# Batch 1's largest logits: VectorE 32x32 squares and five small transfers in place of TensorE transposes and a product with ones

## The chip, the core and the metric

The kernel runs on one core of a Trainium2 chip, with all arithmetic in float32. The metric is the device time in microseconds (us) of one execution, as the median of several runs. Profiles are of one execution; their times start at the beginning of its span.

## What is computed

The reference is four layers on two batches of 1024 tokens of 256 numbers: a cross-attention, a grouped feed-forward layer, a second cross-attention with sigmoids, and a "soft mixture" layer. The change lies in the last one, which in short is:

```
logits   = einsum("bsd,etd->bset", xn, se)        # 1024 tokens x 1024 slots for each batch
dispatch = softmax(logits, axis=1)                # over the tokens
slots    = einsum("bsd,bset->betd", xn, dispatch)
h        = gelu(slots @ w1);  processed = h @ w2
combine  = softmax(logits over all slots, axis=-1)
out      = processed weighted with combine;  x = x + out
```

The softmax over the tokens needs, for every slot, the largest logit of all 1024 tokens of its batch. The logits lie with tokens in partitions, so this is a maximum across partitions, and the result has to be in every partition, since each token's row is reduced by it.

## The kernel before, in words

A batch's 1024 tokens are 8 tiles of 128 tokens. For each tile `logits(b, s)` (line 211) makes 128 x 1024 logits in two PSUM banks on TensorE (L223). VectorE writes their negatives to SBUF (`lg`, L231) and keeps a running elementwise maximum over the tiles (`rmax`, 128 x 1024, L238 and L242). ScalarE makes the exponentials `ec` for the combine step (L246).

After the last tile of a batch `rmax` still holds 128 rows. `largest(b)` (line 289) turns it on TensorE, 8 transposes of 128 x 128 into two banks (`pm`, L295), takes the maximum of each row of the turned squares on VectorE (L296), and writes `dg` on VectorE: eight diagonal 128 x 128 matrices, side by side, with the maxima on the diagonals (L300). `spread(b)` (line 308) multiplies `dg` by a matrix of ones on TensorE (`pb`, L314), which puts the maxima into all partitions, and copies the two banks to `mb`, one half by ScalarE (L170) and one by VectorE (L172).

Then for each tile `less(b, s)` (line 318) adds `mb` to the negative logits on GpSimd (POOL), and `dispatch(b, s)` (line 321) takes the exponential on ScalarE. `gather(b, c)` (line 326) multiplies the exponentials of 128 slots (column `c`) by the tokens: 8 tiles in two passes each, 16 TensorE passes to a column (`psl`, L330). VectorE divides by the sum (`rz`, L338, and `sl`, L340). `turn_slots` (line 343) transposes these slots on TensorE (`pst`, L349), and `slots_out` writes pairs of columns to `slT` (L357). `hidden(b)` runs the first weights and the gelu with seven products in place of eight (L405; its first copy on ScalarE is L438, its first sum on VectorE L445), `processed(b)` the second weights (`pp`, L475), `combined(b)` the combine step (`pc`, L475).

The order of the work: batch 0's `largest`, `spread`, `less` and `dispatch` lie among batch 1's logits. Batch 1's lie after the last logits, where `less(1, c)` and `dispatch(1, c - 1)` are traced with column `c` of batch 0's gather. Batch 1's exponentials are first read by batch 1's gather. `sum_weights` (line 367, four sums on POOL, L373 to L376) prepares the first weights. `turn(q, h)` (line 257) turns halves of `ec` for the combine step: four VectorE transposes in 32 x 32 squares (L275) and 16 transfers on SP's queue (L284). The weights `ms` (2 MB) are loaded on SP's queue (L1270) into memory that becomes free when the logits are done.

A scheduler puts each engine's instructions in order before the run, by readiness in its own model and by order of tracing. The order is then fixed, and an instruction whose input isn't there holds up all behind it on its engine. ScalarE's order is that of the program (L1237). `tc.keep_in_program_order(ins)` pins one instruction behind the instruction of the same engine that was traced before it.

Pools have named memory: tiles of one pool with the same `tag` share it. `slp` has one buffer of the tag `slT`.

Of the kernel before, what the change touches and what calls it, by code (L numbers as in the profile page):

```python
# [9 lines left out]
FP = mybir.dt.float32  # L10
AF = mybir.ActivationFunctionType
ALU = mybir.AluOpType
AX = mybir.AxisListType
PSUM = bass.MemoryType.PSUM

P = 128
# [3 lines left out]
DC = D // P  # L20
# [21 lines left out]
NSLOT = 1024  # L42
# [3 lines left out]
SQ = 32  # L46
R4 = P // SQ
# [3 lines left out]
def tile_kernel(  # L51
# [19 lines left out]
    nc = tc.nc  # L71

    const = ctx.enter_context(tc.tile_pool(name="const", bufs=1))
    stat = ctx.enter_context(tc.tile_pool(name="stat", bufs=4))

    ps = [
        ctx.enter_context(tc.tile_pool(name=f"ps_{i}", bufs=4, space=PSUM)) for i in range(2)
# [2 lines left out]
    def bank(name, side=0):  # L80
        return ps[side].tile([P, 512], FP, tag="bank", name=name)
# [69 lines left out]
    keep, pools = {}, {}  # L151
# [12 lines left out]
    lgs = [[None] * ST for _ in range(B)]  # L164
    ecs = {}
    rmaxs, zcs, mTs, mbs = {}, {}, {}, {}

    def copy(engine, dst, src):
        if engine == 0:
            nc.scalar.copy(dst, src)  # L170
        else:
            nc.vector.tensor_copy(dst, src)  # L172
# [84 lines left out]
    def turn(q, h, late=False):  # L257

        if q < QB:
            tr = pools["m12"].tile(
                [P, R4, EC // 2, QT, SQ], FP, tag="tr", name=f"tr_{q}_{h}", bufs=2
            )
        else:

            if h == 0:
                trs[q] = keep[0].tile(
                    [P, 2, R4, EC // 2, QT, SQ], FP, tag=f"ec_{q % QB}", name=f"tr_{q}"  # L270
                )
            tr = trs[q][:, h]
        half = ecs[q][:, h]
        for t in range(QT):
            ins = nc.vector.transpose(  # L275
                tr[:, :, :, t, :].rearrange("p r c n -> p c r n"),
                half[:, t, :].rearrange("p (c r n) -> p c r n", c=EC // 2, r=R4),
            )
            if late:
                tc.keep_in_program_order(ins)  # L280
        to = half.rearrange("p a b -> p (a b)").rearrange("p (k i n) -> p k i n", i=R4, n=SQ)
        for i in range(R4):
            for r in range(R4):
                nc.sync.dma_start(  # L284
                    out=to[ts(r, SQ), :, i, :],
                    in_=tr[ts(i, SQ), r].rearrange("p c t n -> p (c t) n"),
                )

    def largest(b):

        mT = stat.tile([P, EC], FP, tag="mT", name=f"mT_{b}")
        for h in range(EC // 4):
            pm = bank(f"pm_{b}_{h}", 1)
            for c in range(4):
                nc.tensor.transpose(pm[:, ts(c, P)], rmaxs[b][:, ts(4 * h + c, P)], ident)  # L295
            nc.vector.tensor_reduce(  # L296
                mT[:, ts(h, 4)], pm.rearrange("p (c n) -> p c n", c=4), AX.X, ALU.max
            )
        dg = pools["mw"].tile([P, EC, P], FP, tag="dg", name=f"dg_{b}")
        nc.vector.tensor_tensor(  # L300
            dg,
            ident.unsqueeze(1).to_broadcast([P, EC, P]),
            mT.unsqueeze(2).to_broadcast([P, EC, P]),
            ALU.mult,
        )
        mTs[b] = dg

    def spread(b):

        dgf = mTs[b].rearrange("p c n -> p (c n)")  # L310
        mb = pools["md"].tile([P, NSLOT], FP, tag="mb", name=f"mb_{b}")
        for n in range(NSLOT // 512):
            pb = bank(f"pb_{b}_{n}", 1)
            nc.tensor.matmul(pb, lhsT=ones, rhs=dgf[:, ts(n, 512)], start=True, stop=True)  # L314
            copy(n, mb[:, ts(n, 512)], pb)
        mbs[b] = mb

    def less(b, s):
        nc.gpsimd.tensor_tensor(lgs[b][s], lgs[b][s], mbs[b], ALU.add)  # L319

    def dispatch(b, s):
        nc.scalar.activation(lgs[b][s], lgs[b][s], AF.Exp, scale=-1.0)  # L322
# [3 lines left out]
    def gather(b, c):  # L326

        pz = bank(f"psl_{b}_{c}", 0)
        for s in range(ST):
            nc.tensor.matmul(  # L330
                pz[:, 0:XW],
                lhsT=lgs[b][s][:, ts(c, P)],
                rhs=xhs[b * QB + s // QT][:, s % QT, :],
                start=(s == 0),
                stop=(s == ST - 1),
            )
        rz = stat.tile([P, 1], FP, tag="rz", name=f"rz_{b}_{c}")
        nc.vector.reciprocal(rz, pz[:, D : D + 1])  # L338
        sl = pools["m12"].tile([P, D], FP, tag="sl", name=f"sl_{b}_{c}", bufs=2)
        nc.vector.tensor_scalar(sl, pz[:, 0:D], rz, None, ALU.mult)  # L340
        sls[c] = sl

    def turn_slots(b, c):

        if c % 2 == 0:
            pts[c // 2] = bank(f"pst_{b}_{c // 2}", 1)
        pt = pts[c // 2]
        for dc in range(DC):
            nc.tensor.transpose(  # L349
                pt[:, ds(dc * 2 * P + (c % 2) * P, P)], sls[c][:, ts(dc, P)], ident  # L350
            )
        if c % 2 and c < EC - 1:
            for dc in range(DC):
                slots_out(b, c // 2, dc)
# [12 lines left out]
    def sum_weights():  # L367
        m1s = m12s[0]
        a11, a12 = m1s[:, 0, 0:512], m1s[:, 1, 0:512]
        a21, a22 = m1s[:, 0, 512:], m1s[:, 1, 512:]  # L370
        st = const.tile([P, DC, NSLOT], FP, tag="seT", name="m1_sums")
        s1, s2, s4 = st[:, 0, 0:512], st[:, 0, 512:], st[:, 1, 0:512]
        nc.gpsimd.tensor_tensor(s1, a21, a22, ALU.add)  # L373
        nc.gpsimd.tensor_tensor(a21, a11, a21, ALU.subtract)
        nc.gpsimd.tensor_tensor(s2, s1, a11, ALU.subtract)
        nc.gpsimd.tensor_tensor(s4, a12, s2, ALU.subtract)  # L376
        lefts.extend([a11, a12, s4, a22, s1, s2, a21])
# [310 lines left out]
    with (  # L688
# [349 lines left out]
        with (  # L1038
# [136 lines left out]
            for q in range(NQ):  # L1175
                b = q * QN // S
# [63 lines left out]
    for u in range(1, B * ST + 2):  # L1240
        b, s = divmod(u, ST)
        if b < B:
            if u in (1, 3):
                norm_tokens(QB + u // 2)
                turn_tokens(QB + u // 2)
            logits(b, s)
        v = u - ST
        if v == 1:
            nc.vector.reciprocal(zcs[0], zcs[0])
            largest(0)  # L1250
        if v == 2:
            spread(0)
        if 2 <= v < 2 + ST:
            less(0, v - 2)
        if 3 <= v < 3 + ST:
            dispatch(0, v - 3)
# [1 line left out]
    nc.vector.reciprocal(zcs[1], zcs[1])  # L1258


    largest(1)
    spread(1)
    work.close()
    m12 = open_pool("m12")
    ms = m12.tile([P, DC * FF + OC * D], FP, name="ms")
# [5 lines left out]
    for b in range(B):  # L1271
        slTs[b] = pools["slp"].tile([P, DC, NSLOT], FP, tag="slT", name=f"slT_{b}")
        for c in range(EC):
            gather(b, c)
            if c > 0:
                turn_slots(b, c - 1)
            if b == 0 and c in (1, 3, 5):
                turn(c // 4, c // 2 % 2, c == 5)
            if b == 1 and c % 2 == 0:
                turn(QB + c // 4, c // 2 % 2, True)  # L1280
            if b == 0:
                less(1, c)
                if c > 0:
                    dispatch(1, c - 1)
        if b == 0:
            dispatch(1, ST - 1)
            sum_weights()
        hidden(b)
        with tc.manual_schedule(engines={mybir.EngineType.DVE, mybir.EngineType.PE}):
            processed(b)  # L1290
            combined(b)
# [70 lines left out]
```

## Time and profile before

| | |
|---|---|
| Median of three runs | 444.54 us (443.05 to 444.97) |
| Time of the profiled execution | 443.19 us |
| Its span | 441.4 us |
| TensorE busy (PE) | 430.4 us, 97% |
| VectorE busy (DVE) | 328.4 us, 74% |
| ScalarE busy (ACT) | 114.7 us, 26% |
| GpSimd busy (POOL) | 84.7 us, 19% |
| TensorE's granted clock | 0.999 |
| Logits of both batches, TensorE (L223) | 128 passes, 593 ns each |
| `psl` (L330) | 256 passes, 381 ns each, overlapping |
| `less` on POOL (L319) | 16, 2361 ns each |
| `dispatch` on ScalarE (L322) | 16, 1049 ns each |
| Batch 1's `less` | first one starts at 234.06, last one ends at 252.67 |
| First hidden copy on ScalarE (L438) | 259.98 |

PE is TensorE's products, PEld its weight loads, DVE VectorE, ACT ScalarE, SP the engine that issues the transfers. A line of a timeline gives start, length, engine, line of the kernel, operation, output and inputs, shapes and the number of instructions merged; in brackets stands the idle time before it and what ended it. The chain of waits starts at the last instruction and goes back, at each step, to what released it; a line is start, length and work. A row of a transfer ends in the median time from issue to landing.

### The profile page before, as it was taken

To read this page: it belongs to the slowest core of one execution; us is meant where nothing else is said; L and a number is where in the kernel's file an instruction comes from. 1 tells how busy PE (TensorE), PEld (TensorE's weight loads), DVE (VectorE), ACT (ScalarE), POOL (GpSimd) and SP (SyncE) were. 2 spreads that over 40 slices of the span, in tenths; PEclk is the share of its full clock that TensorE was granted. 3 is DMA by queue.
4 is the path that set the end of the run, shared out by engine and by line. 5 is a ranking of instruction groups with operands and counts; after the bars stand their busy time and mean duration, and the time that the engine had idled before them with its cause. 6 is when DMAs were issued, how large, how long until landed. Compare 5 with 4: busy or idle time off the path is not lost.

```text
span 441.4 us, 6412 instructions
## 1 busy us (share of the span) xinstructions
PE 430.4 (97%) x2368; PEld 319.1 (72%) x2368; DVE 328.4 (74%) x735; ACT 114.7 (26%) x213; POOL 84.7 (19%) x84
## 2 busy tenths in 40 slices
PE   6999999999999999999999999999999999999996
PEld 5788898888645545444458864699998884499996
DVE  0587989899284787998787259995995568796956
ACT  1212334112345441343573405510000002530000
POOL 3012232234212111200887930000000000000000
PEclk9999999999999999999999999999999999999999
DMA  8996595400202132321043633332003666600002
GB/s 269 415 422 274 224 379 206 170 0 7 42 10 39 21 47 30 48 32 18 0 162 72 98 52 50 45 56 43 1 0 103 97 90 99 90 1 1 1 1 97
DMA packets 100641, 42.08 MB, mean 95 GB/s; under 512 B 94593, under 2 KB 96769, under 8 KB 99201
## 3 DMA queue, kind: packets, MB, share of 16 engines
q1 hardware_dynamic: 100610, 41.67, 35.4%
q8 instruction: 19, 0.31, 0.3%
q14 instruction: 12, 0.10, 0.1%
HBM read 28.03 MB, written 2.10 MB: 68 GB/s over the span
## 4 chain that ended last, share of the span: by engine, by line
PE 81%; DVE 15%; POOL 1%; ACT 1%; issue 1%; DMA 1%; ACTq 0%; POOLq 0%
PE psl L330 12%; PE pl L223 12%; PE pp L475 11%; PE pc L475 11%; PE pmh L405 11%; PE pmt L744 5%; DVE b2z L775 5%; PE pq L1120 3%; PE pf L1134 3%; PE psg L1187 2%; PE poT L1221 2%; PE po L802 2%; DVE hn_f L708 1%; DVE bn_f L113 1%; DVE bn_a L113 1%; PE pt_a L125 1%
## 5 line engine op out<-in xcount | busy, mean ns | idle before, releaser
L744 PE MATMUL pmt<-wg 128*128 128x256 f32 x256 | 58.9, 388 | 3.8 <-DMA wg<-in_wff_dram 3.8
L330 PE MATMUL psl<-xh,lg 128*128 128x258 f32 x256 | 58.7, 381 | 0.0
L744 PEld LDWEIGHTS pmt<-wg 128*128 128x128 f32 x256 | 49.2, 195 | 10.7 <-DMA wg<-in_wff_dram 4.1
L223 PE MATMUL pl<-seT,xhT 128*128 128x512 f32 x128 | 55.9, 593 | 0.0
L330 PEld LDWEIGHTS psl<-xh,lg 128*128 128x128 f32 x256 | 47.3, 190 | 7.1 <-issue 0.5
L223 PEld LDWEIGHTS pl<-seT,xhT 128*128 128x128 f32 x128 | 24.2, 190 | 29.1 <-issue 24.9
L319 POOL TENSOR_TENSOR lg<-lg,mb 128x1024 f32<-128x1024 f32 x16 | 37.2, 2361 | 30.8 <-DVE mb L172 30.8
L475 PEld LDWEIGHTS pp<-ms,mh 128*128 128x128 f32 x256 | 29.4, 192 | 1.0 <-issue 1.0
L475 PE MATMUL pp<-ms,mh 128*128 128x128 f32 x256 | 29.7, 276 | 0.0
L246 ACT ACTIVATE ec<-lg,nm 128x1024 f32<-128x1024 f32 x16 | 18.4, 1148 | 40.4 <-DVE nm L231 40.4
L775 DVE SCALAR_TENSOR_TENSOR b2z<-wg,fr,b2z 128x256 f32<-128x256 f32 x48 | 24.6, 516 | 0.5
L415 ACT ACTIVATE mh<-mh 128x512 f32<-128x512 f32 x32 | 19.2, 627 | 20.3 <-DVE mh L448 17.7
L405 PE MATMUL pmh<-slT,ms 128*128 128x512 f32 x48 | 24.0, 592 | 0.0
L475 PE MATMUL pc<-pr,ec 128*128 128x128 f32 x192 | 22.1, 275 | 0.0
L475 PE MATMUL pp<-m_sums,mh 128*128 128x128 f32 x192 | 22.1, 275 | 0.0
L338 DVE RECIPROCAL rz<-psl 128x1 f32<-128x1 f32 x16 | 2.5, 156 | 26.0 <-PE psl L330 26.0
L475 PEld LDWEIGHTS pc<-pr,ec 128*128 128x128 f32 x192 | 21.8, 192 | 0.0
L475 PEld LDWEIGHTS pp<-m_sums,mh 128*128 128x128 f32 x192 | 21.8, 192 | 0.0
L1196 ACT ACTIVATE sg<-psg 128x512 f32<-128x512 f32 x32 | 16.5, 603 | 17.0 <-PE psg L1187 17.0
L275 DVE STREAM_TRANSPOSE tr<-ec 128x512 f32<-128x512 f32 x32 | 20.1, 679 | 0.0
L322 ACT ACTIVATE lg<-lg 128x1024 f32<-128x1024 f32 x16 | 16.5, 1049 | 12.4 <-POOL lg L319 12.4
L486 DVE TENSOR_TENSOR mh<-mh,mh 128x1024 f32<-128x1024 f32 x16 | 18.5, 1219 | 1.5 <-PE pp L475 1.5
(187 smaller groups left out, 703.9 us busy)
## 6 DMA issues: line engine op xcount, KB each, us to landing
wg<-in_wff_dram SPq DMA_DIRECT2D x6, 2048.0 KB, 14.3
ec<-tr SPq DMA_DIRECT2D x128, 64.0 KB, 2.3
xT<-in_xT_dram SPq DMA_DIRECT2D x4, 512.0 KB, 12.8
x<-in_x_dram SPq DMA_DIRECT2D x4, 512.0 KB, 15.0
wg<-in_wff_dram SPq DMA_DIRECT2D x2, 1024.0 KB, 10.6
xhT<-tr_m SPq DMA_DIRECT2D x64, 32.0 KB, 2.0
ms<-in_m_dram SPq DMA_DIRECT2D x1, 2048.0 KB, 7.9
out_dram<-x SPq DMA_DIRECT2D x16, 128.0 KB, 1.8
```

The costliest lines, as they stand in the source:

```text
L223: nc.tensor.matmul(pl, lhsT=xhTs[q][:, dc, ts(t, P)], rhs=seT[:, n, dc, :], start=(dc == 0), stop=(dc == DC - 1),)
L246: nc.scalar.activation(ecs[q][:, :, t, :], lg.rearrange("p (h n) -> p h n", h=2), AF.Exp, bias=nm[:, 1:2], scale=-1.0, accum_out=zcs[b][:, ...
L275: ins = nc.vector.transpose(tr[:, :, :, t, :].rearrange("p r c n -> p c r n"), half[:, t, :].rearrange("p (c r n) -> p c r n", c=EC // 2, ...
L319: nc.gpsimd.tensor_tensor(lgs[b][s], lgs[b][s], mbs[b], ALU.add)
L322: nc.scalar.activation(lgs[b][s], lgs[b][s], AF.Exp, scale=-1.0)
L330: nc.tensor.matmul(pz[:, 0:XW], lhsT=lgs[b][s][:, ts(c, P)], rhs=xhs[b * QB + s // QT][:, s % QT, :], start=(s == 0), stop=(s == ST - 1),)
L405: nc.tensor.matmul(to, lhsT=lefts[i][:, ts(j, P)], rhs=slTs[b][:, i, 0:512] if i < 2 else rights[b][i], start=True, stop=True,)
L415: nc.scalar.activation(h, h, AF.Gelu)
L475: nc.tensor.matmul(to, lhsT=left(k, m), rhs=right[:, k, :], start=(k == 0), stop=(k == QT - 1),)
L486: nc.vector.tensor_tensor(dst, x, y, op)
L744: nc.tensor.matmul(pm[:, ts(hc, D)], lhsT=w1g[:, oc, ts(hc, P)], rhs=w2g[:, oc, :], start=(oc == 0 and hc == 0), stop=(oc == OC - 1 and hc ...
L775: nc.vector.scalar_tensor_tensor(acc, weights[g][1][:, oc, :], b1s[:, g, oc : oc + 1], acc, ALU.mult, ALU.add)
```

## The change

For batch 1 alone `largest` and `spread` are replaced. `largest_by_moves` transposes `rmax` on VectorE in 32 x 32 squares, so that in each block of 32 partitions the partition number stands for the slot within a square; the maximum over the 32 numbers of each square leaves `m1`, 128 x 32. Four transfers bring the four blocks of 32 partitions side by side into 32 partitions (`m4`). `spread_by_moves` takes the maximum over the four (`m2`), turns that 32 x 32 square (`m3`), writes it to DRAM as one row of 1024 numbers, and reads that row into all 128 partitions (`mb`).

The working memory `w` is a tile of the tag `slT`, the one that `slT_0` uses afterwards. `spread_by_moves(1)` is traced in the loop over batch 0's columns behind `gather(0, 0)`; its first reduce is pinned behind the VectorE instruction traced before it. `sum_weights` moves from behind that loop to the same place, ahead of `less(1, 0)`. Of batch 1's `less`, tiles 3 and 6 go to VectorE.

```diff
+    dram = ctx.enter_context(tc.tile_pool(name="dram", bufs=1, space=bass.MemoryType.DRAM))
...
+    moved = {}
+
+    def largest_by_moves(b):
+
+        w = pools["slp"].tile([P, DC, NSLOT], FP, tag="slT", name=f"max_{b}")
+        sq = w[:, 0, :]
+        nc.vector.transpose(sq, rmaxs[b])
+        m1 = w[:, 1, 0:SQ]
+        nc.vector.tensor_reduce(m1, sq.rearrange("p (c k) -> p c k", k=SQ), AX.X, ALU.max)
+        m4 = w[0:SQ, 1, SQ : 5 * SQ].rearrange("n (i c) -> n i c", i=R4)
+        for i in range(R4):
+            nc.sync.dma_start(out=m4[:, i, :], in_=m1[ts(i, SQ), :])
+        moved[b] = w, m4
+
+    def spread_by_moves(b):
+
+        w, m4 = moved[b]
+        m2, m3 = w[0:SQ, 1, 5 * SQ : 6 * SQ], w[0:SQ, 1, 6 * SQ : 7 * SQ]
+        tc.keep_in_program_order(
+            nc.vector.tensor_reduce(m2, m4.rearrange("n i c -> n c i"), AX.X, ALU.max)
+        )
+        nc.vector.transpose(m3, m2)
+        row = dram.tile([SQ, SQ], FP, name=f"mrow_{b}")
+        nc.sync.dma_start(out=row, in_=m3)
+        mb = pools["md"].tile([P, NSLOT], FP, tag="mb", name=f"mb_{b}")
+        nc.sync.dma_start(out=mb, in_=row.rearrange("c n -> (c n)").partition_broadcast(P))
+        mbs[b] = mb
+
     def less(b, s):
-        nc.gpsimd.tensor_tensor(lgs[b][s], lgs[b][s], mbs[b], ALU.add)
+        engine = nc.vector if b == 1 and s in (3, 6) else nc.gpsimd
+        engine.tensor_tensor(lgs[b][s], lgs[b][s], mbs[b], ALU.add)
...
-    largest(1)
-    spread(1)
+    largest_by_moves(1)
     work.close()
...
+            if b == 0 and c == 0:
+                spread_by_moves(1)
+                sum_weights()
             if b == 0:
                 less(1, c)
                 if c > 0:
                     dispatch(1, c - 1)
         if b == 0:
             dispatch(1, ST - 1)
-            sum_weights()
```

## The prediction

> **What bounds the kernel now.** I read the page first, then the chain of waits around the change and behind it, then the timeline of the stretch by engine, and last the rows that carry the costs. The chain says that from the change to the end nothing but TensorE counts:
>
> ```profile
> 225.83 0.02 issue
> 225.86 0.75 DVE lg L231
> ...
> 228.13 0.68 DVE mT L296
> 228.81 0.02 issue
> 228.83 2.26 DVE dg L300
> 231.09 0.04 issue
> 231.14 1.98 PE pb L314 x4
> 233.12 3.49 PE psl L330 x16
> 236.61 0.22 PE pst L349 x2
> ```
>
> ```profile
> 333.62 6.98 PE psl L330 x32
> 340.60 0.22 PE pst L349 x2
> ```
>
> The first fence (start, length, what) is where the chain leaves TensorE: batch 0's gather has begun, but batch 1's maxima go VectorE, `dg`, then TensorE's product with ones. From the last logits' end (225.83) to the first slot transpose (236.61) batch 0 needs 10.78 us; batch 1, with the same 32 passes of `psl` and nothing between, needs 6.98 us. All after 236.61 is TensorE work end to end, so each microsecond saved here moves the end, if nothing new stops TensorE. The timeline of the engines in that stretch:
>
> ```profile
> 225.69 0.63 PE L295 MATMUL pm<-ident,rmax 128*128 128x128 f32 x4
> 226.16 1.47 PE L330 MATMUL psl<-xh,lg 128*128 128x258 f32 x6
> 227.47 0.60 PE L295 MATMUL pm<-ident,rmax 128*128 128x128 f32 x4
> 227.90 2.56 PE L330 MATMUL psl<-xh,lg 128*128 128x258 f32 x10
> 231.14 1.98 PE L314 MATMUL pb<-dg,ones 128*128 128x512 f32 x4 [0.67 <-DVE dg L300]
> 232.96 3.65 PE L330 MATMUL psl<-xh,lg 128*128 128x258 f32 x16
> ```
>
> **What is removed.** On TensorE 8 transposes and 4 passes of `pb` with the idle time before them: at most 10.78 - 6.98 = 3.80 us. On VectorE two reduces, `dg` and half of `mb` (0.68 + 0.69 + 2.25 + 0.69 = 4.3 us), on ScalarE a copy of 0.59. How much of the 3.80 comes out depends on the gather's other input, the exponentials of batch 0:
>
> ```profile
> 227.80 3.88 ACT L322 ACTIVATE lg<-lg 128x1024 f32<-128x1024 f32 x4
> ```
>
> They end at 231.68, the last four 0.97 apart, and are not touched by the change. If TensorE went through column 0 to its end before column 1, it would finish column 0 at 231.68 + 2 x 0.22 = 232.1 and column 1 at 235.6, for a gain of only 1.0. But 16 passes were done by 230.46, before that last exponential, so they can't be all of column 0: the order already mixes columns. Mixed, four passes of tile 7 are left at 231.68, which ends at 232.55, before the 232.81 (225.83 + 6.98) that TensorE needs anyway. I take 0.3 off for imperfect mixing.
>
> **What is added, and when the maxima arrive (T).** VectorE ends its last maximum at 226.53 + 0.68 = 227.2; the reciprocal of `zc` takes 0.2. The 128x1024 square transpose is two rows of L275 (128x512, 0.679) or less, 1.25; the reduce is the row of L861 (128x4 from 128x1024, 1.22). So `m1` is there at 229.9. Four transfers follow on SP's queue. Their issue costs 0.34 each (the row of `ms`) to 0.63 (L284), their landing 2.0 to 2.3:
>
> ```profile
> ec<-tr SPq DMA_DIRECT2D x128, 64.0 KB, 2.3
> xhT<-tr_m SPq DMA_DIRECT2D x64, 32.0 KB, 2.0
> ms<-in_m_dram SPq DMA_DIRECT2D x1, 2048.0 KB, 7.9
> out_dram<-x SPq DMA_DIRECT2D x16, 128.0 KB, 1.8
> ```
>
> `ms` was issued at 225.85, when its memory came free, before `m1` exists, and lands at 233.75; the moves stand behind its bytes: 233.3 at best, 234.6 at worst, I take 234.4. The small reduce and transpose are between 0.16 each (VectorE's 128x4 rows) and 0.68 (a 512-element row); I take 0.5 together, 234.9. The row goes to DRAM in 1.8 to 2.3: 236.9. Reading it back as 128 x 4 KB has no row near: 2.0, and 0.5 MB at (7.9 - 2.0)/2 MB gives 3.5; `bo_bc`, the only like read, took 8.2 in the crowded start. The Trainium skill, "DMA: Bandwidth & Descriptors", section "Anatomy of one DMA", has 2.0 us and bytes over 436 GB/s, which would be 3.2; by the same rule `ms` would take 6.8, the trace shows 7.9, so I stay with the trace. With 0.5 for transfers of `turn` in between, T = 240.9, between 239.5 and 245. The old maxima were there at 233.9. That is 7 us later, and what hides it is that batch 1's exponentials are used first in batch 1's gather at 333.
>
> Three covers have to hold (TensorE's work taken 3.0 earlier than now):
> - The small reduce is pinned behind column 0's slots and waits for the moves until 234.4. Queued behind it are column 1's `rz` and `sl` (0.7), so done by 235.6; TensorE wants them at 239.94 - 3.0 = 236.9. Free; each us after 235.7 costs one. Slots 0 are written into the memory that holds the squares, so they wait for the row's transfer: at 237.9 against 236.9, free as well.
> - POOL now does the weight sums first (252.64 to 257.85, 5.2 us): from 233.75 to 239.0, before T, so free. Then six `less` of 2.33 while VectorE takes two. The last exponential ends at T + 6 x 2.33 + 2 x 1.22 + 1.06 = T + 17.5 = 258.4. ScalarE keeps program order, so the first copy of the hidden layer stands behind it. VectorE needs that copy at 263.88, so it may start as late as 263.25 - 3.0 = 260.2: 1.8 of slack, good up to T = 242.7.
> - Two `less` on VectorE, tiles 3 and 6. Undisturbed 128x1024 sums take 1.22 (L486). But:
>
> ```profile
> L300 DVE TENSOR_TENSOR dg<-ident,mT x2: 1221/1736/2252, 206.3 to 228.8; 128x1024 f32<-128x1024 f32 x2
> ```
>
> The second `dg` took 2.25 because POOL's last `less` ran until 230.0: 1.17 of waiting and 1.22 of work. At 99.80 two POOL sums in a row let one VectorE instruction through between them. The Trainium skill, "SBUF — State Buffer", section "Who interferes with whom", says why: a VectorE instruction with two SBUF inputs and a GpSimd one that reads SBUF share a port, one holding it for its whole instruction. By L486's row a `less` costs VectorE 1.22; by the rule up to 2.33 + 1.22 = 3.55, and the waiting falls on the `rz` and `sl` queued behind. A column's `rz` (244.06 for column 3, its slots wanted at 247.36, 0.7 of work) can slip 2.6 us for nothing. One `less` ahead of column 3 (rz due 241.0, at the latest 243.7) frees VectorE at T + 1.22 or T + 3.55, 242.1 or 244.5: a stall of 0 or 0.8. I take 0.4, and 0.3 for slips of columns 0 to 2.
>
> **Sum.** 3.80 - 0.3 - 0.4 - 0.3 = 2.8 us gained. The profiled execution took 443.19 (span 441.4 and 1.8 around it), which gives 440.4; the median of the three runs is 444.54, so 441.7.
>
> **Rivals.**
> - *Both `less` stand together on VectorE ahead of one column's `rz`* (the slower side). They become ready at the same moment, which speaks for it; against it, columns' `rz` come every 3.7 us and were traced earlier. VectorE is then free at T + 4.8 (it gets the port first) or T + 7.1 (POOL first), 245.7 or 248.0 against the 243.7 that column 3 allows: 2.0 to 4.3 of stall. With 3.5 left of the gain before it, that is -1.5 to +0.8 at my T, and each us of T adds one: with POOL first it is slower than before from T = 240.1 and by 2.2 (0.5%) from T = 242.3, inside the bounds of T; with VectorE first only from 242.4. I price it at POOL first and 242.3: 446.7.
> - *The row or the broadcast is queued behind `turn`'s transfers.* VectorE is idle while it waits, so the 16 transfers of a `turn` may be ready before the row. SP issues one per 0.66 (32 in 21.4 us from 236.85), 16 are 10.6. T would be 251, column 3 stalls 251 + 1.2 + 0.7 - 244.4 = 8.5 or more: 444.5 - 3.5 + 8.5, about 449.5. Against it: the row needs SP before most of them do.
> - *Little comes out*: columns in order (gain 1.0), or the stall of a `less` eats most: 443.5.
>
> **Chances.** Forecast 0.54, 441.7 (its own range 440.5 to 442.8); little 0.22, 443.5; both together 0.15, 446.7; queued behind 0.09, 449.5. The range 440.4 to 446.7 leaves out the last case, half of the third and a little below. A measurement of this kernel tells 0.5% (2.2 us) from no change. Of the forecast 0.45 is under 442.3, with 0.05 of "little" 0.5 faster; the third case splits at its T, so same 0.3, slower 0.2.
>
> **What would show it.** Right: the chain runs from logits to `psl` without `pm` and `pb`; the first 32 `psl` passes end near 233; POOL's first `less` starts near 241; the last exponential ends before 260; `pst` never waits for `sl`. Wrong: idle time of TensorE before `pst` released by VectorE's `sl`, with a `less` of over 2 us on VectorE before it; the broadcast issued after 238; a wait of TensorE or VectorE for the first `mh` copy.

## The result and the profile after

The changed kernel takes 440.76 us (median of six runs, 439.91 to 441.36), the kernel before 444.36 (six runs, 443.05 to 444.97). The ratio is 0.9922 with a 95% interval of 0.9905 to 0.9940, a gain of 2.7 to 4.2 us. The forecast was 441.7. (The title counts five transfers. There are six: four moves, the row to DRAM and its broadcast back.)

Lines below the new functions have moved: `psl` is now L360, `pst` L379, `pmh` L435, `less` L349 on both engines, `slT` L387, and the four sums of slots that the hidden layer's products need L422 to L426. The profiled execution took 441.36, with a span of 439.6; before it was 443.19 and 441.4. In this execution the last logits end at 227.06, 1.23 later than before. That lies at the kernel's start: its first 32 products (`pmt`) took 10.26 us in the place of 8.93. In two later profiles with the change the logits end at 225.93 and 226.07. So times of the two kernels are compared from the end of the logits.

First the chain of waits around the change (start, length, what):

```profile
227.06 8.36 PE psl L360 x38
235.42 0.22 PE pst L379 x2
235.64 2.18 PE psl L360 x10
237.82 0.22 PE pst L379 x2
...
257.44 0.23 PE pst L379 x2
257.68 0.02 issue
257.70 0.88 DVE slT L387 x2
258.57 2.04 DVE sl_sums L422
260.61 0.14 issue
260.75 4.53 PE pmh L435 x10
```

The detour over VectorE, `pm` and `pb` is gone, and TensorE goes from logits to `psl` without a stop. The second `pst` comes 10.76 after the logits (237.82 - 227.06); before it came 14.49 after them. That is 3.73 gained, of at most 3.80. Then, at 257.68, the chain leaves TensorE in a place where it did not before: a sum of slots on VectorE takes 2.04 where such a sum takes 0.68. From the end of the logits to the first product of batch 0's combine step (`pc`) it is 80.49 us, before 82.78: of the 3.73 gained only 2.29 are left. Behind that point nothing differs: from there to the start of VectorE's last instruction it is 129.04 or 129.05 in the profile of before and in each one below.

The points in the kernel before (the second `pst` and the first `pc` of its chain, then the same sum of slots on VectorE's timeline), and the first `pc` of the changed kernel:

```profile
240.32 0.22 PE pst L349 x2
...
308.61 25.01 PE pc L475 x224
```

```profile
260.99 0.68 DVE L392 TENSOR_TENSOR sl_sums<-slT 128x512 f32<-128x512 f32 x1
```

```profile
307.55 25.01 PE pc L505 x224
```

VectorE and POOL in the same stretch (start, length, engine, line, work; in brackets the idle time before and what ended it):

```profile
231.38 2.48 DVE L276 STREAM_TRANSPOSE tr<-ec 128x512 f32<-128x512 f32 x4
...
236.48 0.32 DVE L338 TENSOR_REDUCE max<-max 32x32 f32<-32x128 f32 x1
...
245.36 2.21 DVE L349 TENSOR_TENSOR lg<-lg,mb 128x1024 f32<-128x1024 f32 x1
...
248.67 2.19 DVE L349 TENSOR_TENSOR lg<-lg,mb 128x1024 f32<-128x1024 f32 x1
...
258.49 2.11 DVE L422 TENSOR_TENSOR sl_sums<-slT 128x512 f32<-128x512 f32 x1
260.63 0.69 DVE L424 TENSOR_TENSOR sl_sums<-slT,sl_sums 128x512 f32<-128x512 f32 x1
```

```profile
235.27 1.31 POOL L403 TENSOR_TENSOR m_sums<-ms 128x512 f32<-128x512 f32 x1 [4.04 <-DMA max<-max]
...
244.13 15.91 POOL L349 TENSOR_TENSOR lg<-lg,mb 128x1024 f32<-128x1024 f32 x6 [3.62 <-DMA mb<-mrow]
```

POOL's six subtractions start when the broadcast lands, at 244.13, and end at 260.04. The first sum of slots on VectorE starts at 258.49, while POOL's last subtraction runs, and ends at 260.60, 0.56 after it: about 1.5 of waiting and the rest of work. The second sum, started behind POOL's end, takes its 0.69. TensorE was idle for 1.37 in front of the product that needs the first sum. This is the sharing that the forecast had read off `dg`, at a place that the forecast had not looked at.

SP's queue, and the transfers' time from issue to landing (the last column of the second fence):

```profile
231.54 2.48 SPq L330 DMA_DIRECT2D max<-max  x4
...
237.06 0.34 SPq L342 DMA_DIRECT2D mrow<-max  x1
237.45 1.27 SPq L285 DMA_DIRECT2D ec<-tr  x2
239.01 0.37 SPq L344 DMA_DIRECT2D mb<-mrow  x1
```

```profile
mb<-mrow SPq DMA_DIRECT2D x1, 512.0 KB, 5.1
...
max<-max SPq DMA_DIRECT2D x4, 4.0 KB, 2.9
...
mrow<-max SPq DMA_DIRECT2D x1, 4.0 KB, 1.9
```

Only two transfers of `turn` came between the row and the broadcast, while the row was still on its way. The broadcast itself is the long one.

How the 2.29 of the trace stand to the 3.6 between the medians: from the start of VectorE's last instruction to the end of the span it is 3.75 before and 3.01 after, which makes 3.0. Nothing in the change touches that end, and in the other profiles below it lies between 2.9 and 4.7, so I count it as scatter, like the start. The changed kernel run once more beside the first experiments gained 2.0 to 3.5 (ratio 0.9938, 0.9921 to 0.9955). The interval of that run holds the 2.3 of the trace, with or without that end. The interval of the first, 2.7 to 4.2, holds it only with that end, so part of the 3.6 is not accounted for.

### The profile page after: what moved, and what is told of

Same layout as the page of the kernel before. It is cut to its first block, busy times and chain, and to the rows that moved or that the text cites. A ratio compares the mean times of both kernels' runs of the same rounds, so it can differ in the third digit from the quotient of the medians.

```text
span 439.6 us, 6389 instructions
## 1 busy us (share of the span) xinstructions
PE 428.7 (98%) x2356; PEld 318.5 (72%) x2356; DVE 332.0 (76%) x737; ACT 113.7 (26%) x212; POOL 81.9 (19%) x82
## 4 chain that ended last, share of the span: by engine, by line
PE 81%; DVE 14%; POOL 1%; ACT 1%; DMA 1%; issue 1%; ACTq 0%; POOLq 0%
PE psl L360 13%; PE pl L224 12%; PE pp L505 11%; PE pc L505 11%; PE pmh L435 11%; PE pmt L774 5%; DVE b2z L805 5%; PE pq L1150 3%; PE pf L1164 3%; PE psg L1217 2%; PE poT L1251 2%; PE po L832 2%; DVE hn_f L738 1%; DVE bn_f L114 1%; DVE bn_a L114 1%; PE pt_a L126 1%
## 5 line engine op out<-in xcount | busy, mean ns | idle before, releaser
L774 PE MATMUL pmt<-wg 128*128 128x256 f32 x256 | 60.3, 394 | 3.8 <-DMA wg<-in_wff_dram 3.8
L360 PE MATMUL psl<-xh,lg 128*128 128x258 f32 x256 | 58.2, 381 | 0.0
L360 PEld LDWEIGHTS psl<-xh,lg 128*128 128x128 f32 x256 | 47.4, 190 | 7.2 <-issue 0.5
L349 POOL TENSOR_TENSOR lg<-lg,mb 128x1024 f32<-128x1024 f32 x14 | 34.5, 2501 | 30.4 <-DVE mb L173 26.7
L435 PE MATMUL pmh<-slT,ms 128*128 128x512 f32 x48 | 24.2, 592 | 0.0
```

What stands on the lines that cost most here:

```text
L349: engine.tensor_tensor(lgs[b][s], lgs[b][s], mbs[b], ALU.add)
L360: nc.tensor.matmul(pz[:, 0:XW], lhsT=lgs[b][s][:, ts(c, P)], rhs=xhs[b * QB + s // QT][:, s % QT, :], start=(s == 0), stop=(s == ST - 1),)
L435: nc.tensor.matmul(to, lhsT=lefts[i][:, ts(j, P)], rhs=slTs[b][:, i, 0:512] if i < 2 else rights[b][i], start=True, stop=True,)
L774: nc.tensor.matmul(pm[:, ts(hc, D)], lhsT=w1g[:, oc, ts(hc, P)], rhs=w2g[:, oc, :], start=(oc == 0 and hc == 0), stop=(oc == OC - 1 and hc ...
```

## The experiments

My theory after the result: the gain is TensorE's own removed work and the wait for `dg`, 3.7 us; about 1.4 of it is given back, since POOL's subtractions last until the sums of slots, and VectorE's sums wait for POOL there. Rivals: the gain comes from the early weight sums or from the split of the subtractions, which are also in the change; it is the wait for `dg` alone; or VectorE and ScalarE gain from being relieved.

For each run the table gives its ratio to the kernel before, which ran beside it, with its 95% interval, and what its trace gains against the kernel before from the end of the logits to the second `pst`, and to the first `pc`. What a kernel gains in the first and not in the second it gave back later.

| Run | Median, us | Ratio | Gain to second `pst` | Gain to `pc` |
|---|---|---|---|---|
| changed kernel | 440.76 | 0.9922 (0.9905 to 0.9940) | 3.73 | 2.29 |
| changed kernel again | 440.63 | 0.9938 (0.9921 to 0.9955) | 3.73 | 2.33 |
| old maxima, other parts new | 443.91 | 1.0009 (0.9997 to 1.0021) | 0.01 | 0.01 |
| all subtractions on POOL (`c1_pool_only`) | 443.15 | 1.0004 (0.9989 to 1.0020) | 3.73 | 0.05 |
| old maxima, wait covered (`c1_spread_later`) | 443.99 | 1.0014 (1.0005 to 1.0023) | 0.94 | -0.73 |
| same, `turn` moved too | 442.78 | 0.9975 (0.9965 to 0.9986) | 0.93 | 0.92 |
| third subtraction on VectorE (`c2_third_on_vector`) | 439.19 | 0.9902 (0.9886 to 0.9918) | 3.73 | 3.72 |
| second trip by way of DRAM | 441.75 | 0.9958 (0.9944 to 0.9972) | 3.73 | 1.38 |
| third, and `turn` held back | 440.44 | 0.9928 (0.9914 to 0.9943) | 3.73 | 2.49 |
| third, again | 439.55 | 0.9906 (0.9889 to 0.9922) | 3.73 | 3.70 |
| third, with products put back | 442.68 | 0.9986 (0.9972 to 1.0000) | 1.98 | 0.70 |
| both batches by moves, two steps twice | 443.81 | 1.0005 (0.9996 to 1.0014) | see below | |
| both batches by moves | 439.69 | 0.9908 (0.9893 to 0.9923) | see below | |

**The changed kernel again**, as the base of the next three:

> The changed kernel once more, so that the other kernels of this set have it beside them. My theory (the products and transposes of batch 1's maxima no longer stand in TensorE's queue): 3.0 to 3.7 us under the kernel before, 440.8. Any rival must give the same here.

It gained 3.0 between the medians, and its trace shows the same 3.73 and 2.33.

**The other parts alone.** The maxima go the old way; the early weight sums and the split subtractions stay:

```diff
-    largest_by_moves(1)
+    largest(1)
+    spread(1)
...
-                spread_by_moves(1)
                 sum_weights()
```

> The kernel before with everything of the change except the moves: the weight sums ahead of the subtractions, and tiles 3 and 6 subtracted on VectorE, but maxima by transposes and the product with ones. My theory: no gain, 444.4 within 0.7, since TensorE's queue is as before. The rival that the gain comes from the shorter chain on POOL and the earlier sums: 441 to 442.

No gain, 0.01 on the chain. By themselves these two parts are worth nothing.

**All subtractions on POOL.** The maxima go the new way, but the split is undone:

```diff
-        engine = nc.vector if b == 1 and s in (3, 6) else nc.gpsimd
+        engine = nc.gpsimd
```

> The changed kernel with all eight subtractions of batch 1 on POOL. They then end 8 x 2.33 after T, 244.1 + 18.6 = 262.8 against 260.0. My theory: the last exponential ends at 263.9 and the first hidden copy 2.8 later than now, and VectorE's slot sums meet POOL's port twice; 1.5 to 3.5 us slower than the changed kernel, 442.3 to 444.3. The rival that the tail on POOL is still hidden: same as the changed kernel, 440.8.

As expected: the 3.73 to the second `pst` are all there and nearly all lost again. Its chain shows where:

```profile
258.08 2.40 DVE sl_sums L422
260.48 0.02 issue
260.50 2.73 DVE sl_sums L424
```

Two sums of slots, of 0.68 each when undisturbed, wait for POOL, which is at its subtractions until 262.67. So the two subtractions on VectorE, worthless alone, carry 2.2 of the changed kernel's gain. What limits the change is when POOL is done, not TensorE.

**Old maxima, wait covered.** The kernel before, with `spread(1)` traced behind `gather(0, 0)` and its first product pinned there, so that the gather runs while VectorE makes `dg`; to give `dg` memory that is free then, it lies in a tile of the tag `slT`:

```diff
-    spread(1)
...
+            if b == 0 and c == 0:
+                spread(1)
```

> The kernel before with its TensorE work unchanged, but the product with ones pinned behind column 0's passes, and dg in other memory. TensorE then doesn't wait for dg. My theory (2.6 of the 3.8 are TensorE's own passes, 1.2 the wait): 225.83 + 0.87 + 1.72 + 6.98 = 235.4 for the first slot transpose in place of 236.6, a gain of 1.2, 443.2. The rival that the wait was all of it: a gain of 3 or more, 441. A third reading, that the wait only moves: 444.4.

A miss in time and a hit in the stretch itself: 0.94 were gained up to the second `pst`, but the scheduler, given another order of tracing, put four transposes of `turn` ahead of the sums of slots, and TensorE waited for those:

```profile
258.56 2.48 DVE tr L275 x4
```

**The same, with that `turn` moved** behind the first sums of the hidden layer:

```diff
-            if b == 0 and c in (1, 3, 5):
+            if b == 0 and c in (1, 3):
...
+            if b == 0 and j == 0:
+                turn(1, 0, True)
```

> As c1_spread_later (the kernel before, its product with ones pinned behind column 0's passes), but with the four transposes of the third turn traced inside the hidden layer, where VectorE did them in the kernel before; in c1_spread_later they had slipped ahead of the slot sums and cost 1.6 again. My theory: what c1_spread_later had gained at the first slot transpose (0.94) now reaches the end: 0.9 to 1.2 under the kernel before, 442.7. The rival that a wait of TensorE taken away here always comes back: no gain, 443.7.

As expected, 442.78. The wait for `dg` is worth 0.93 of the 3.73. The other 2.8 are TensorE's own instructions: the 8 `pm` (0.95 in this run's chain) and the 4 `pb` (1.72) make 2.67. The rival of the wait alone falls.

**A third subtraction on VectorE**, to have POOL done before the sums of slots; VectorE's three are pinned in the order of tracing:

```diff
-        engine = nc.vector if b == 1 and s in (3, 6) else nc.gpsimd
-        engine.tensor_tensor(lgs[b][s], lgs[b][s], mbs[b], ALU.add)
+        engine = nc.vector if b == 1 and s in (3, 4, 6) else nc.gpsimd
+        ins = engine.tensor_tensor(lgs[b][s], lgs[b][s], mbs[b], ALU.add)
+        if engine is nc.vector:
+            tc.keep_in_program_order(ins)
```

> The changed kernel with three subtractions of batch 1 on VectorE (tiles 3, 4 and 6), each pinned behind the slots of its own column. POOL then ends about 1.1 sooner (5 x 2.33 + 3 x 1.22 of the shared port in place of 6 x 2.33 + 2 x 1.22), 258.9 against 260.0. My theory (1.4 are lost where POOL's last subtraction holds the port against the first slot sum): 0.7 to 1.2 faster than the changed kernel, 439.7. The rival that the loss there is the wait for the first hidden copy or for the weights: no gain, 440.7; if VectorE's queue becomes the bound: slower.

It gained somewhat more than that: 439.19, and all of the 3.73 arrives at `pc`. Its POOL, and its first sum of slots on VectorE:

```profile
243.01 14.58 POOL L349 TENSOR_TENSOR lg<-lg,mb 128x1024 f32<-128x1024 f32 x5 [3.40 <-DMA mb<-mrow]
```

```profile
257.50 0.68 DVE L424 TENSOR_TENSOR sl_sums<-slT 128x512 f32<-128x512 f32 x1
```

POOL ends at 257.59, the sum starts at 257.50 and takes 0.68. The three subtractions on VectorE took 2.07, 2.20 and 2.27, and TensorE waited for none. This is faster than both kernels of the study. It also takes the loss at 258.5 to POOL, and not to the memory or to the products' order, which are the same.

**A second trip by way of DRAM**, to move the arrival of the maxima alone:

```diff
+        row2 = dram.tile([SQ, SQ], FP, name=f"mrow2_{b}")
+        nc.sync.dma_start(out=row2, in_=row)
...
-        nc.sync.dma_start(out=mb, in_=row.rearrange("c n -> (c n)").partition_broadcast(P))
+        nc.sync.dma_start(out=mb, in_=row2.rearrange("c n -> (c n)").partition_broadcast(P))
```

> The changed kernel with one more transfer, from DRAM to DRAM, between the row and the broadcast. T is 2.5 to 3 later. My theory (T has used up its slack): POOL ends near 262.7, two slot sums wait for the port as in c1_pool_only; 2 to 3 us slower than the changed kernel, 443.2. The rival that the transfers are hidden with room: same, 440.7.

The direction was right, the size too large. The extra trip took 2.36, but the broadcast behind it took 4.1 in the place of 5.1, so that POOL started only 1.3 later (18.41 after the logits, against 17.07). The chain lost 0.91 of its gain, and a sum of slots waited again (the second one, 2.72). Over this 1.3 a microsecond of delay of the maxima cost about 0.7.

**The third subtraction, and `turn` held back** on SP's queue until the broadcast is issued, with a `turn` moved as above:

```diff
+                if q == 0:
+                    tc.add_manual_dep(
+                        move.ins,
+                        moved["mb"].ins.name,
...
```

> The changed kernel with three subtractions on VectorE and the first turn's transfers held on SP's queue until the broadcast is issued, and the third turn traced in the hidden layer. My theory: the broadcast took 5.1 because the turn's transfers share its engines; alone it takes 3.5 to 4, and T comes 1.5 to 2.5 sooner. POOL ends before the slot sums, nothing is lost there: 1.2 to 1.6 under the changed kernel, 439.3. The rival that the broadcast is slow by itself: as c2_third_on_vector.

A miss that split in two. The hold takes away the transfers of `turn` that were issued ahead of the row and of the broadcast; the others follow right behind it:

```profile
237.29 0.34 SPq L351 DMA_DIRECT2D mb<-mrow  x1
237.68 21.62 SPq L285 DMA_DIRECT2D ec<-tr  x32
```

The broadcast fell from 5.0 to 3.8, and POOL started 15.31 after the logits, against 16.94 without the hold. So the hold did speed the way up, and what it changed are the transfers issued ahead; those issued behind the broadcast were there in both runs. They are not the whole cause: in the run with the second trip two stood ahead as well, and the broadcast took 4.1.

The rest went wrong at VectorE's third subtraction. It stands in the same place, ahead of column 7's `rz` and `sl`, and starts 27.02 after the logits in both runs. It took 3.03 in the place of 2.27 (first fence without the hold, second with it; VectorE, then the subtraction that POOL was at):

```profile
253.09 2.27 DVE L349 TENSOR_TENSOR lg<-lg,mb 128x1024 f32<-128x1024 f32 x1
...
251.92 2.36 POOL L349 TENSOR_TENSOR lg<-lg,mb 128x1024 f32<-128x1024 f32 x1
```

```profile
252.91 3.03 DVE L356 TENSOR_TENSOR lg<-lg,mb 128x1024 f32<-128x1024 f32 x1
...
252.48 2.37 POOL L356 TENSOR_TENSOR lg<-lg,mb 128x1024 f32<-128x1024 f32 x1
```

POOL's had begun 1.17 before VectorE's without the hold, and 0.43 before it with the hold, so VectorE waited longer for POOL's end. This is the stall of the forecast's slower rival, with one subtraction and another column. Of the 1.2 lost up to `pc` 0.5 is there at the next `pst`. The other 0.7 went in and behind the hidden layer, where the four transposes of the moved `turn` came behind nine sums in the place of five; no run takes the two apart. The earlier arrival gained nothing, since without it nothing was late any more.

**The third subtraction again, and with products put back.** The second kernel puts two products with ones (4 passes) ahead of the gather, whose results nobody reads:

```diff
+    for n in range(NSLOT // 512):
+        pb = bank(f"ballast_{n}", 1)
+        nc.tensor.matmul(pb, lhsT=ones, rhs=rmaxs[1][:, ts(n, 512)], start=True, stop=True)
     work.close()
```

> The changed kernel with a third of batch 1's subtractions (tile 4) on VectorE once more, as the base of the two runs beside it: 439.2 again, within 0.5.

> The same kernel with two products with ones put back on TensorE ahead of the gather (4 passes of 128x512, the size of those that the change removed; nobody reads them, nothing waits for them). Theory that the gain is TensorE's own time: the 4 passes took 1.98 in the kernel before, so 2.0 slower than the kernel without them, 441.2; and the wait for dg, which isn't put back, stays gained. Rival that the gain came from VectorE and ScalarE, relieved of dg and of the copies of mb: no change, 439.2.

The base was 439.55, the other 442.68: 3.1 slower, not 2.0. Up to the second `pst` it lost 1.75, from these passes:

```profile
226.99 0.97 PE ballast L1296 x2
227.96 0.87 PE psl L362 x4
228.84 0.86 PE ballast L1296 x2
...
255.84 3.21 DVE lg L349
```

The first term is as the theory had it: the passes cost what they take, about 0.45 each. The last line is what it had not. The third subtraction stands ahead of column 7 in the base too; but the columns come 1.75 later here and the maxima only 0.3, so that POOL's subtraction had begun 0.16 before it, not 1.13, and it took 3.30 in the place of 2.33 (3.21 of it in the chain). At the next `pst` another 0.75 was lost, and 0.5 more up to `pc`, where VectorE's order in the hidden layer differs again. So the rival of VectorE and ScalarE relieved isn't needed for the gain, but the difference between the medians is not a clean measure of the passes.

**Both batches by moves.** Batch 0's largest logits go the new way too, `less(0, s)` and `dispatch(0, s)` come one tile later, and tiles 2 and 5 are subtracted on VectorE. By an oversight the first of these kernels subtracts the maximum from tile 6 of batch 0 twice and takes tile 5's exponential twice, which the reference does not; the second does each once.

```diff
-            largest(0)
-        if v == 2:
-            spread(0)
-        if 2 <= v < 2 + ST:
-            less(0, v - 2)
...
+            largest_by_moves(0)
+        if v == 3:
+            spread_by_moves(0)
+        if 3 <= v < 2 + ST:
+            less(0, v - 3)
...
```

> The same kernel with batch 0's largest logits brought by squares and transfers as well; batch 0's subtractions are placed one tile later and two of them (tiles 2 and 5) go to VectorE. TensorE loses 8 transposes (1.04) and 4 passes (1.88), 2.9 us. In the run with three subtractions the old path has batch 0's maxima on all partitions at 211.6; by the 16 us that batch 1's path took, less the bytes of the weights that stood in its way, the new one has them at about 216.5. POOL's six subtractions then end near 230.7 against 230.2 and the last exponential near 232.3 against 231.9, just in time for the gather: if that holds, 436.5 to 437. Rival: the exponentials come 2 us or more later and TensorE waits for them at the gather, where nothing hides it, each microsecond costing one: 439 or slower.

> Both batches' largest logits by squares and transfers, as in the run before, which by an oversight subtracted batch 0's maximum from tile 6 twice and took tile 5's exponential twice; here each is done once. That takes one subtraction of 2.34 off POOL ahead of the last exponential, and one exponential of 1.0 off ScalarE. If TensorE's wait of 3.12 before the last passes of columns 0 and 1 is for POOL's last subtraction, the whole 2.34 comes out: 441.5, still about 2 slower than the kernel with only batch 1 moved (439.4). Rival: the wait is for something else (the order of the gather's passes) and 443.8 stays; or the old estimate was right but for the oversight, and 437 comes.

The first took 443.81, the second 439.69, no different from the base with one batch moved (439.55). Both expectations of the second were missed: it is 1.8 faster than the theory had it, and 2.7 slower than the first estimate. TensorE in the second kernel, and in the first:

```profile
226.12 7.46 PE L362 MATMUL psl<-xh,lg 128*128 128x258 f32 x32 [1.34 <-ACT lg L354]
234.31 2.44 PE L362 MATMUL psl<-xh,lg 128*128 128x258 f32 x10 [0.73 <-ACT lg L354]
```

```profile
236.80 3.88 PE L362 MATMUL psl<-xh,lg 128*128 128x258 f32 x10 [3.12 <-ACT lg L354]
```

The maxima of batch 0 arrive at 217.24 in the second kernel, against 211.50 in the base: 5.7 later. Batch 0's exponentials are needed at once by the gather, and TensorE waits for them, 1.34 and 0.73, 2.07 together. The logits end 2.02 earlier than in the base. So what TensorE saves it waits for, and the trade gives nothing. From the first to the second kernel the long wait shrank by 2.39, as one subtraction of 2.34 would have it. The other part is in the ten passes behind it, 3.88 and 2.44. The granted clock explains them (columns: stretch, length, busy time of TensorE, weight loads, VectorE, ScalarE and POOL, clock, share of the transfers, GB/s), in the first kernel:

```profile
234.00:237.00 3.00, 0.20 (x1) 0.20 (x2) 0.92 (x2) 1.31 (x2) 2.92 (x3) 1.00 0.30 44
237.00:241.00 4.00, 4.00 (x13) 3.06 (x13) 1.70 (x6) 0.69 (x1) 3.73 (x3) 0.60 0.00 0
```

After an idle time of 3.12 TensorE was granted 0.60 of its clock on the mean over the next 4 us. In the second kernel, after 0.73, it was 1.00. (By the Trainium skill, "TensorE: Matmul & The Clock Gate", section "Part 1: The HAM clock gate", the clock is halved after an idle window of about 3.4 us; here 3.12 was enough.)

## Why the prediction was right, and where by luck

The forecast of 441.7 was 0.9 above the median, in its own range of 440.5 to 442.8. Its sum of 2.8 is near the 2.29 of the chain, but not by its own terms.

- *At most 3.80 on TensorE.* Right: 3.73, of which 2.8 are instructions and 0.93 the wait.
- *0.3 off for imperfect mixing of columns.* Not needed. The second `pst` lost 0.07 in all.
- *0.4 for a subtraction on VectorE and 0.3 for slips of columns 0 to 2.* Not needed. The subtractions took 2.21 and 2.19, between the row's 1.22 and the rule's 3.55, and no `pst` waited for `sl`. They came to stand ahead of different columns, so the slower rival did not come about. The run with `turn` held back shows the price where a subtraction ahead of an `rz` waits longer for POOL: 0.5 at the next `pst`.
- *Cover of the last exponential, good until T = 242.7.* This is the step that failed. T was 244.13, or 242.9 in the times of the kernel before, 2.0 later than forecast. The exponentials still came in time (their last one ends at 261.14, 259.9 in the old times), and the hidden layer's first copy held up nobody. But the cover was tested on ScalarE's side alone. POOL's last subtraction lasted until 260.04, and the sums of slots on VectorE, due at 258.5, share the port with it. That cost 1.43 of the 3.73. The forecast weighed the port rule of the Trainium skill, "SBUF — State Buffer", section "Who interferes with whom", for the two subtractions on VectorE, and not for VectorE's other instructions with two SBUF inputs in POOL's time. At the sums the rule holds: one waits for the rest of one of POOL's instructions, 0.68 becoming 2.11 here and 2.40 and 2.73 with everything on POOL. At the forecast's T of 240.9 POOL's six subtractions (15.91) would have ended at 256.8, and the sums come at 257.3 (258.5 - 1.23). By this estimate the cost comes from the 2.0 by which T was late, and the room ended at T = 241.4 (257.3 - 15.9), not at 242.7.
- *T itself.* In the times of the kernel before: `m1` at 230.2 (forecast 229.9). The last of the four moves landed at 234.6 (234.4). `m3` at 235.8 (234.9): the small reduce stood behind a transpose of `turn` on VectorE until 236.48, 235.25 in the old times, a queue that the forecast had watched on SP and not on VectorE. Row landed at 237.7 (236.9), as forecast about 2 from its issue. The broadcast took 5.1, not 3.5 and 0.5 for transfers of `turn` in between, and that is the largest term. With `turn`'s transfers ahead of it held back it was 3.8, near the forecast's 3.5 from `ms`; batch 0's broadcast in the last run, with no `turn` near it, took 3.6. The Trainium skill's figure, worked out as an estimate of 3.2 in the prediction from "Anatomy of one DMA", is the page's fit for transfers that GpSimd issues; these were issued by SP.
- *Pinned reduce, slots 0 behind the row, weight sums first on POOL: free.* Right; POOL was idle for 3.62 between the weight sums and its first subtraction.
- *Rival of the row behind `turn`'s transfers.* Two of these came between, and hid behind the row's own way. Its cause was real in another form: not SP's turn, but what was under way when the broadcast was issued.

So an overcautious 1.0 and an overlooked 1.43 nearly cancelled, and that is luck. What stays open: the ends of the executions, 2.9 to 4.7 us behind the start of VectorE's last instruction, and their starts differ by a microsecond from run to run, and no run here says why. Open is also why the broadcast took 5.0 to 5.3 in some runs and 3.9 to 4.1 in others, with two transfers of `turn` ahead of it in all of them.

## What to carry to other kernels

Where TensorE is the bound, a reduction across partitions can leave it for VectorE squares and small transfers, if nobody needs the result for as long as the way takes: about 17 us here from the last logits, hidden for batch 1 once POOL had three subtractions less, and no gain for batch 0. When an engine's work is moved later, list everything that the other engine does in those microseconds, not only who waits for its result; here the moved subtractions met sums that have nothing to do with them. And after each small edit look at the order and the times of the other instructions before reading its time: in one of these runs four transposes that nobody had edited moved ahead of sums that TensorE needed, and in two a subtraction that stayed in its place met POOL at another moment and waited longer.

## What was not expected of the hardware

- A row of 4 KB in DRAM read into 128 partitions (512 KB) took 5.0 to 5.3 us in six runs behind two transfers of 64 KB, 3.9 to 4.1 in three others behind two such, 3.8 with none issued ahead of it, and 3.6 with none near it.
- VectorE and POOL, both on sums with two SBUF inputs, let each other through one instruction at a time. A sum of 1.22 on VectorE took 2.27, 3.03 and 3.30 when POOL's current one of 2.36 had begun 1.17, 0.43 and 0.16 before it. Two that got in with POOL's first took 1.22 and 1.23, and POOL's then took 3.40. Sums of 0.68 took up to 2.73.
- TensorE's granted clock fell to 0.60 after an idle time of 3.12 and cost 1.44 in ten passes; after idle times of 0.73 to 1.73 the profiles show 1.00. Yet with all subtractions on POOL, where idle times of 1.73 and 1.66 follow each other, five of the 22 executions show a mean clock of 0.992 and took 446.0 to 446.5, against a median of 443.15. Their profiles were not kept, so the cause is open.
